# A two-expert MoE layer on one core: the experts last, their weighted rows added to the result in memory

## The chip, the cores and the metric

The kernel runs on one core of one Trainium2 chip. The time is the device time of that core in microseconds, from launch to end of one execution. The kernel before takes 1065.1 us, the median of three runs (1060.12, 1065.28 and 1065.1). Five engines matter: TensorE (PE in the profile; its weight loads are PEld), VectorE (DVE), ScalarE (ACT), GpSimd (POOL) and SyncE (SP). Each runs its own list of instructions strictly in order and waits on semaphores. DMAs are started from SyncE, ScalarE or GpSimd and are carried out by 16 DMA engines; a DMA whose rows are addressed by a list of indices (indirect) is started from GpSimd.

## The reference

Eight sequences of 256 tokens (2048 in all) of width 1024, float32. Each sequence has an adapter matrix; its product y goes through a mixture of experts with a shared part, and the result is added to x:

```python
y = einsum('bsi,boi->bso', x, cond_weight[itok])            # adapter by sequence
g, u = split(y @ shared_w_gate_up.T, 2)                     # 1024 each
shared = (silu(g) * u) @ shared_w_down.T
probs = softmax(y @ gate_w.T)                               # 16 experts
vals, idx = top_k(probs, 2); vals /= vals.sum(-1)
for each expert e:                                          # 256 inner, gate and up
    out_e = (silu(g_e) * u_e) @ w_down[e].T
out = x + shared + sum over the two experts of vals * out_e
```

## The kernel before

**Arithmetic.** Products are float32 in effect: each operand is split into a high and a low part (`split`, L58, a cast on ScalarE at L59 and a subtraction on VectorE at L60), and `mm3` (L73) makes three TensorE products for each. A weight tile of 128x1024 is loaded from SyncE into one of four `wst` buffers and split into one of seven `whl` buffers (`load_w`, L64).

**Stages.** The token blocks are 128 rows, and four of them make a group; there are four groups.

1. `cond` (L145), once for each sequence: y = adapter product, written to `y_d` in memory from ScalarE's queue.
2. `group_yt` (L469): reads y of a group back from GpSimd's queue and transposes it. `route` (L171): gate products, softmax, the two best experts, their weights `c1` and `c2`, and each token's rank within its expert. With it, indirect DMAs of one number a token scatter the token's place in `y_d` into a table `tab_d`, sorted by expert (L268). The index tile `sli` of that scatter has one buffer. A table of the weights goes to `comb_d`.
3. `shared_up` (L284) and `shared_down` (L307) for a group: 384 and 192 products. The order is group 0, interleaved with stages 1 and 2, then group 3, then the experts, then groups 1 and 2.
4. Before the experts, small VectorE work sorts the experts by their number of tokens and computes, for each token and each of its two experts, the row in `os_d` where that expert's output row will be (`s1i`, `s2i`, L546 to L556).
5. `experts` (L457) goes through the 16 experts, the fullest first. Each has a fixed capacity (`CAPS`, 304 down to 256 tokens). `expert_rows` (L431) loads the expert's table entries (`ib`) from SyncE, makes the addresses (`segments`, L425, on GpSimd) and gathers y in pieces of 128 rows x 256 (`gather_rows`, L345, L351). `expert_yt` transposes them, `expert_up` (L384) makes the 96 up products, `expert_down` (L396) and, for tokens from 256 on, `expert_down_last` (L412) make 24 or 32 down products. `expert_out` (L449) writes the rows to `os_d` from SyncE. On TensorE the up products of expert n+1 stand ahead of the down products of expert n. Output tiles `o` have three buffers, gathered rows `yg` four.
6. `combine` (L328) gathers, for a token block, the two rows from `os_d` (L331) and adds them with their weights on VectorE (L337). For groups 1 and 2 it adds into the tile that the shared network is then added to. Groups 0 and 3 had gone to `xs_d` before the experts; `combine_kept` (L339) reads them back, combines and writes them to `out`, between the up products of group 1 and of group 2.
7. Tokens beyond an expert's capacity are handled by `rest` (L579) in a loop at the end. With these inputs no expert has any.

**Order.** The program is written in this sequence; a scheduler, which is given a simulated timeline (L650), decides how instructions of different steps are interleaved on each engine. Buffers that are in use, and the last load (`issue_after`), hold later steps back.

Of the kernel before, what the change touches and what calls it, by code (L numbers as in the profile page):

```python
# [9 lines left out]
F32 = mybir.dt.float32  # L10
# [16 lines left out]
# tokens computed in the main pass for the fullest expert, the next one, ...; what is past them comes after it  # L27
# [4 lines left out]
ROW0 = [sum(CAPS[:n]) for n in range(E + 1)]  # L32
ZROW = ROW0[E]
PAD = 4 * T


@with_exitstack
def adapter_moe_kernel(ctx: ExitStack, tc: tile.TileContext, xT, x, itok, wc, gate, wgu, wd, sgu, sd, out):
# [14 lines left out]
    comb_d = dram.tile([T + P, E], F32, tag="comb_d", name="comb_d")  # L53
    tab_d = dram.tile([E * SLOTS, 1], I32, tag="tab_d", name="tab_d")
    os_d = dram.tile([ZROW + 16, H], F32, tag="os_d", name="os_d")
    xs_d = dram.tile([T, H], F32, tag="xs_d", name="xs_d")
# [27 lines left out]
    tid = cpool.tile([P, T // P], I32, tag="tid", name="tid")  # L84
    rev = cpool.tile([P, NB, E], F32, tag="rev", name="rev")
    caps = cpool.tile([P, E], F32, tag="caps", name="caps")
    row0 = cpool.tile([P, E], F32, tag="row0", name="row0")
    oneh = [cpool.tile([P, T // P, E], BF, tag=f"oneh{r}", name=f"oneh{r}") for r in range(2)]
    ranks = [cpool.tile([P, T // P], F32, tag=f"ranks{r}", name=f"ranks{r}") for r in range(2)]
    # hi/lo of the gate for each chunk; a stationary block runs on into the next chunks, whose products aren't used  # L90
    gpk = cpool.tile([P, (NC - 1) * 2 * E + P], FR, tag="gpk", name="gpk")
    s1i = cpool.tile([P, T // P], I32, tag="s1i", name="s1i")
    s2i = cpool.tile([P, T // P], I32, tag="s2i", name="s2i")
    c1 = cpool.tile([P, T // P], F32, tag="c1", name="c1")
    c2 = cpool.tile([P, T // P], F32, tag="c2", name="c2")
# [3 lines left out]
    def constants():  # L99
# [5 lines left out]
        nc.gpsimd.iota(tid, pattern=[[4 * P, T // P]], base=0, channel_multiplier=1)  # L105
# [6 lines left out]
        for j in range(E):  # L112
            nc.gpsimd.memset(row0[:, j : j + 1], float(ROW0[j] - ZROW))
# [12 lines left out]
        nc.sync.dma_start(comb_d[T : T + P, :], zr[:, :E])  # L126
        nc.sync.dma_start(os_d[ZROW : ZROW + 16, :], zr[:16, :])
        ti = rows.tile([P, 1024], I32, tag="yg", bufs=4, name="ti")
        nc.gpsimd.memset(ti[:, : E * SLOTS // P], PAD)
        nc.sync.dma_start(tab_d.rearrange("(p f) o -> p (f o)", p=P), ti[:, : E * SLOTS // P])  # L130

    # r: partition (a, i), column (t, c), 32 rows i of each t, segment a of 256 columns of a row
    # -> hi/lo of the transpose at columns off:off+n of yt [P, 2, NC, *]; partition (a, j) of
    # chunk b holds column 256a + 32b + j
# [36 lines left out]
    def route(g, yt):  # L171
# [44 lines left out]
        v.tensor_tensor(c1[:, gs], m[0], den, op=ALU.mult)  # L216
        v.tensor_tensor(c2[:, gs], m[1], den, op=ALU.mult)
        cb = t3("cb")
        v.tensor_tensor(cb, oh[0], bc(c1[:, gs]), op=ALU.mult)
        v.tensor_tensor(key, oh[1], bc(c2[:, gs]), op=ALU.mult)  # L220
        v.tensor_tensor(cb, cb, key, op=ALU.add)
        nc.scalar.dma_start(comb_d[g * GT : (g + 1) * GT, :].rearrange("(k p) e -> p k e", p=P), cb)
# [24 lines left out]
        for r in range(2):  # L247
            rank = ranks[r][:, gs]
            sl, sli, tq, ov, u = t2("sl"), t2("sli", I32), t2("tq"), t2("ov"), t2("u")
            v.tensor_copy(oneh[r][:, gs, :], oh[r])  # L250
            v.tensor_tensor(key, rk, oh[r], op=ALU.mult)
            v.tensor_reduce(rank, key, axis=AX.X, op=ALU.add)
            # place of rank 32t + i: 8i + t below MAIN, the rank itself from MAIN on
            v.tensor_scalar(ov, rank, float(MAIN), None, op0=ALU.is_lt)
            v.tensor_scalar(tq, rank, -15.5, 1.0 / 32, op0=ALU.add, op1=ALU.mult)
            v.tensor_copy(sli, tq)
            v.tensor_copy(tq, sli)
            v.tensor_scalar(u, rank, 7.0, None, op0=ALU.mult)
            v.scalar_tensor_tensor(u, tq, -255.0, u, op0=ALU.mult, op1=ALU.add)
            v.tensor_tensor(u, u, ov, op=ALU.mult)  # L260
            # expert = E - kk
            v.tensor_scalar(sl, kk[r], -float(SLOTS), float(SLOTS * E), op0=ALU.mult, op1=ALU.add)
            v.tensor_tensor(sl, sl, rank, op=ALU.add)
            v.tensor_tensor(sl, sl, u, op=ALU.add)
            v.tensor_copy(sli, sl)
            for k in range(NB):
                tb = g * NB + k
                nc.gpsimd.indirect_dma_start(  # L268
                    out=tab_d[:, :],
                    out_offset=bass.IndirectOffsetOnAxis(ap=sli[:, k : k + 1], axis=0),  # L270
                    in_=tid[:, tb : tb + 1],
                    in_offset=None,
                )
# [54 lines left out]
    def combine(tb, a):  # L328
        for si, cw in ((s1i, c1), (s2i, c2)):
            r = rows.tile([P, 1024], F32, tag="yg", bufs=4, name="r")  # L330
            nc.gpsimd.indirect_dma_start(  # L331
                out=r,
                out_offset=None,
                in_=os_d[:, :],
                in_offset=bass.IndirectOffsetOnAxis(ap=si[:, tb : tb + 1], axis=0),
            )
            nc.vector.scalar_tensor_tensor(a, r, cw[:, tb : tb + 1], a, op0=ALU.mult, op1=ALU.add)  # L337

    def combine_kept(tb):  # L339
        a = rows.tile([P, 1024], F32, tag="o", name="kept")  # L340
        nc.sync.dma_start(a, xs_d[tb * P : (tb + 1) * P, :])
        combine(tb, a)
        nc.sync.dma_start(out[tb * P : (tb + 1) * P, :], a)

# [51 lines left out]
    def expert_down(at, w, off):  # L396
        o = rows.tile([P, 1024], F32, tag="o", name="o")
        for h in range(2):
# [9 lines left out]
            nc.scalar.copy(o[:, h * 512 : (h + 1) * 512], ps)  # L408
        return o

    # a3: hi of n tokens at columns 0.., lo at 64..; the products' halves are added after
    def expert_down_last(a3, w, n):  # L412
        o = rows.tile([P, 1024], F32, tag="o", name="ol")
        for h in range(2):
# [6 lines left out]
            nc.vector.tensor_tensor(o[:n, hs], ps[:n, :], o[:n, hs], op=ALU.add)  # L421
        return o[:n, :]

    # ib: places in y of 32 rows for each t -> those of their four segments
# [5 lines left out]

    def expert_rows(n):  # L431
        e = expert_id(n)
        last = CAPS[n] - MAIN
        nt = -(-last // 32)
        ib = sml.tile([32, 10], I32, tag="ib", name="ib")
        nc.sync.dma_start(ib[:, :8], tab_d[ds(e * SLOTS, MAIN), :].rearrange("(i t) o -> i (t o)", t=8))
        for t in range(nt):
            nc.sync.dma_start(ib[:, 8 + t : 9 + t], tab_d[ds(e * SLOTS + (MAIN + 32 * t), 32), :])
        ix = segments(ib, 8 + nt)
# [9 lines left out]
    def expert_out(n, at):  # L449
        w = load_wd(expert_id(n))  # L450
        r0 = ROW0[n]
        for j in range(2):
            nc.sync.dma_start(os_d[r0 + j * P : r0 + (j + 1) * P, :], expert_down(at, w, j * P))
        if CAPS[n] > MAIN:
            nc.sync.dma_start(os_d[r0 + MAIN : r0 + CAPS[n], :], expert_down_last(at3[n % 2], w, CAPS[n] - MAIN))

    def experts(yt, rs, after):  # L457
        at = expert_up(0, yt)
        for n in range(E):
            yt = expert_yt(rs) if n + 1 < E else after()  # L460
            if n + 2 < E:
                rs = expert_rows(n + 2)
            prev = at
            if n + 1 < E:
                at = expert_up(n + 1, yt)
            expert_out(n, prev)
        return yt

    def group_yt(g):  # L469
        yt = big.tile([P, 2, NC, GT], FR, tag="big", name="yt")  # L470
        for k in range(NB):
            r = rows.tile([P, 1024], F32, tag="yg", bufs=4, name="yr")
            # token 4i + t of the block at (t, i)
# [19 lines left out]
    shared_down(0, ht, acc, xs_d, (0,))  # L493
# [6 lines left out]
    shared_down(0, ht, acc, xs_d, (1,))  # L500
    route(3, yt)
    # tokens per expert
# [13 lines left out]
    # experts by their number of tokens, the fullest first  # L516
    rev1 = rev[:, 0, :]
    cnt, pos, sq = once("cnt", [P, E]), once("pos", [P, E]), rows.tile([P, E, E], F32, tag="o", name="sq")
    perm, red, capof = once("perm", [P, E, E], BF), once("red", [P, E]), once("capof", [P, E])
# [6 lines left out]
    # perm[n, e]: expert e is the n-th  # L526
# [4 lines left out]
    v.tensor_tensor(sq, perm, by_row(caps[:, :]), op=ALU.mult)  # L531
    v.tensor_reduce(capof, sq.rearrange("p n e -> p e n"), axis=AX.X, op=ALU.add)
    # blocks of P tokens past its capacity, for the n-th, and their sum: ceil(k / P) = rint((k + 63.5) / P)
# [10 lines left out]
    # row of the experts' results, by token; the row of zeros for a rank past the capacity  # L544
    v.tensor_tensor(sq, perm, by_row(row0[:, :]), op=ALU.mult)
    v.tensor_reduce(pos, sq.rearrange("p n e -> p e n"), axis=AX.X, op=ALU.add)  # L546
    for r, si in enumerate((s1i, s2i)):
        lim, row = once("lim", [P, T // P]), once("row", [P, T // P])
        v.tensor_tensor(sq, oneh[r], by_col(capof[:, :]), op=ALU.mult)
        v.tensor_reduce(lim, sq, axis=AX.X, op=ALU.add)  # L550
# [103 lines left out]
```

## Time and profile before

| What | Value |
|---|---|
| runs | 1060.12, 1065.28, 1065.1 us; median 1065.1 |
| profiled execution | span 1060.8 us, from its first to its last instruction |
| TensorE | 1029.5 us busy, 5181 products; mean clock 0.992 |
| VectorE, ScalarE, GpSimd | 657.7, 466.4, 292.1 us busy |
| DMA | 243.86 MB, 230 GB/s in the mean |
| queue started from SyncE (q1) | 186.46 MB, 52.6% of the 16 engines' span |
| queue started from GpSimd (q0) | 47.87 MB, 13.0% |
| HBM | 203.11 MB read, 39.69 MB written |

The span is 0.7 us above the lowest run and 4.3 below the median. In the profile's lists, `L60 DVE TENSOR_TENSOR hl<-st,hl` is line 60's instruction on VectorE that writes `hl` from `st` and `hl`. Tiles: `st` and `hl` are weights as loaded and as split, `eps` and `ops` the experts' up and down sums, `sps` and `dps` those of the shared network, `cps` those of the adapters, `yte` an expert's transposed rows, `xacc` a block of x to which results are added. A busy TensorE counts a product from start to modelled end, so neighbours overlap; products of 512 columns follow one another every 0.23 us. In a table by stretches, the columns after the length are busy microseconds of each engine with the number of instructions, then the granted TensorE clock, the mean busy share of the DMA engines and GB/s.

### The profile page before, as it was taken

How to read it: one execution, taken by the hardware profiler on the slowest of the kernel's cores; microseconds unless marked ns; L12 is line 12 of the kernel's file. 1: busy time of each engine (PE TensorE's matmuls, PEld its weight loads, DVE VectorE, ACT ScalarE, POOL GpSimd, SP SyncE). 2: the span in 40 equal slices, each digit the busy share in tenths (PEclk: the TensorE clock that was granted, in tenths of full speed). 3: DMA queues.
4: the chain of work that ended last, by engine and by line, in shares of the span. 5: the costliest groups of instructions: out<-in, count | busy, mean ns of one | idle time of the engine just before them, and what ended most of it. 6: DMA issues, size and time to landing. Idle time of an engine off the chain costs nothing.

```text
span 1060.8 us, 14494 instructions
## 1 busy us (share of the span) xinstructions
PE 1029.5 (97%) x5181; PEld 875.8 (83%) x5181; DVE 657.7 (62%) x918; ACT 466.4 (44%) x626; POOL 292.1 (28%) x332
## 2 busy tenths in 40 slices
PE   6989999999899899999999999999999999999997
PEld 5877888888677688889999999989988888888886
DVE  5676543765567745546877878777784768537321
ACT  5564342544344423314667666566473233122200
POOL 1000210001200223644666656545203423002000
PEclk9999999999899999999999999999999999999999
DMA  7986384567677443655788888787979987827201
GB/s 257 345 301 219 105 253 140 204 232 215 223 249 253 135 159 88 220 189 186 237 283 275 291 271 282 249 273 251 340 262 358 408 344 264 318 92 258 80 33 50
DMA packets 82557, 243.86 MB, mean 230 GB/s; under 512 B 14204, under 2 KB 23164, under 8 KB 82476
## 3 DMA queue, kind: packets, MB, share of 16 engines
q1 hardware_dynamic: 56060, 186.46, 52.6%
q0 software_dynamic: 15856, 47.87, 13.0%
q10 hardware_dynamic: 10560, 8.52, 2.4%
q8 instruction: 42, 0.69, 0.2%
q14 instruction: 39, 0.32, 0.1%
HBM read 203.11 MB, written 39.69 MB: 229 GB/s over the span
## 4 chain that ended last, share of the span: by engine, by line
PE 57%; DMA 5%; issue 5%; POOL 3%; DVE 3%; ACT 1%; POOLq 0%; DVEq 0%; ACTq 0%
PE sps L76 8%; PE sps L75 8%; PE sps L74 8%; PE dps L76 4%; PE dps L75 4%; PE dps L74 4%; PE eps L76 4%; PE eps L74 4%; PE eps L75 4%; POOL yg L351 3%; PE ops L76 2%; PE ops L75 1%; DMA y_d<-yrow 1%; PE ops L74 1%; PE ops L419 1%
## 5 line engine op out<-in xcount | busy, mean ns | idle before, releaser
L60 DVE TENSOR_TENSOR hl<-st,hl 128x1024 fp32r<-128x1024 f32 (+1 forms) x274 | 330.1, 1209 | 180.0 <-ACT hl L59 178.9
L59 ACT CAST hl<-st 128x1024 fp32r<-128x1024 f32 (+1 forms) x274 | 283.5, 1043 | 254.8 <-PE sps L76 79.0
L76 PE MATMUL sps<-yt,hl 128*128 128x512 f32 x512 | 199.5, 390 | 0.0
L75 PE MATMUL sps<-yt,hl 128*128 128x512 f32 x512 | 199.4, 389 | 0.0
L74 PE MATMUL sps<-yt,hl 128*128 128x512 f32 x512 | 198.9, 390 | 0.0
L351 POOL DMA_INDIRECT yg<-y_d,ix x128 | 149.9, 1171 | 40.1 <-issue 35.1
L74 PE MATMUL eps<-yte,hl 128*128 128x256 f32 (+6 forms) x512 | 147.6, 289 | 0.1
L76 PE MATMUL eps<-yte,hl 128*128 128x256 f32 (+6 forms) x512 | 147.5, 288 | 0.0
L75 PE MATMUL eps<-yte,hl 128*128 128x256 f32 (+6 forms) x512 | 147.0, 287 | 0.0
L76 PEld LDWEIGHTS sps<-yt,hl 128*128 128x128 f32 x512 | 96.1, 188 | 20.0
L74 PEld LDWEIGHTS sps<-yt,hl 128*128 128x128 f32 x512 | 96.2, 188 | 19.9
L75 PEld LDWEIGHTS sps<-yt,hl 128*128 128x128 f32 x512 | 96.1, 188 | 19.9
L74 PE MATMUL cps<-hl 128*128 128x512 f32 x256 | 100.8, 398 | 7.6 <-ACT hl L59 7.6
L75 PE MATMUL cps<-hl 128*128 128x512 f32 x256 | 102.2, 399 | 3.2 <-DVE hl L60 3.2
L76 PE MATMUL cps<-hl 128*128 128x512 f32 x256 | 101.7, 397 | 0.0
L76 PE MATMUL dps<-hl,ht 128*128 128x512 f32 x256 | 99.8, 390 | 0.0
L75 PE MATMUL dps<-hl,ht 128*128 128x512 f32 x256 | 99.6, 389 | 0.0
L74 PE MATMUL dps<-hl,ht 128*128 128x512 f32 x256 | 99.6, 389 | 0.0
L74 PEld LDWEIGHTS eps<-yte,hl 128*128 128x128 f32 x512 | 96.4, 188 | 1.1 <-DVE s L378 0.5
L75 PEld LDWEIGHTS eps<-yte,hl 128*128 128x128 f32 x512 | 96.5, 188 | 0.7
L76 PEld LDWEIGHTS eps<-yte,hl 128*128 128x128 f32 x512 | 96.3, 188 | 0.0
L474 POOL DMA_DIRECT2D yr<-y_d x24 | 13.4, 559 | 239.9 <-DMA y_d<-yrow 189.7
(153 smaller groups left out, 1307.5 us busy)
## 6 DMA issues: line engine op xcount, KB each, us to landing
st<-sgu SPq DMA_DIRECT2D x64, 512.0 KB, 3.7
st<-wgu SPq DMA_DIRECT2D x64, 512.0 KB, 3.8
st<-wc SPq DMA_DIRECT2D x63, 512.0 KB, 4.7
st<-sd SPq DMA_DIRECT2D x32, 512.0 KB, 3.9
st<-wd SPq DMA_DIRECT2D x32, 512.0 KB, 5.2
os_d<-o SPq DMA_DIRECT2D x32, 512.0 KB, 5.7
yr<-y_d POOLq DMA_DIRECT2D x24, 512.0 KB, 6.3
y_d<-yrow ACTq DMA_DIRECT2D x16, 512.0 KB, 8.9
```

Of the source, the lines that this page charges most:

```text
L59: nc.scalar.copy(hi, src)
L60: nc.vector.tensor_tensor(lo, src, hi.bitcast(F32), op=ALU.subtract)
L74: nc.tensor.matmul(ps, lhs[0], rhs[0], start=first, stop=False)
L75: nc.tensor.matmul(ps, lhs[0], rhs[1], start=False, stop=False)
L76: nc.tensor.matmul(ps, lhs[1], rhs[0], start=False, stop=last)
L351: nc.gpsimd.indirect_dma_start(out=r[:, t * 256 : (t + 1) * 256], out_offset=None, in_=y_d.rearrange("k a p f -> (k a p) f"), in_offset=ba ...
L419: nc.tensor.matmul(ps, a3[:, fi, :], w[fi][:, l, hs], start=(fi == 0 and l == 0), stop=(fi == 1 and l == 1))
L474: nc.gpsimd.dma_start(r, y_d[g * NB + k].rearrange("a (i t) f -> (a i) (t f)", t=4))
```

## The change

The experts come after all four groups of the shared network. The order is group 0, 3, 1, 2, then the experts, the one with the fewest tokens first. All shared results go to `out` at once; `xs_d`, `os_d`, `comb_d`, `combine` and `combine_kept` are gone.

A table entry grows from one number to four (`ENT`): the token's place in `y_d`, its weight for this expert, its row in `out`, and an unused one. Empty entries name one of 256 extra rows (`DUMMY`) at the end of `out`, which the result leaves out. The table is in plain order of rank, and the step that permuted ranks below 256 is gone. Before the experts, `entries` loads the numbers of all 16 experts from SyncE (two or three DMAs for each): the places with 32 to a column (`ibs`), and whole entries with one to a partition (`ews`).

`expert_down` scales by the weight when ScalarE copies the sums out; `expert_down_last` multiplies on VectorE. `add_out` then starts, from GpSimd, an indirect DMA that adds the tile's rows to rows of `out` in memory. An expert's adds wait for all adds of the expert before it; those of one expert do not wait for each other. In the built order the adds of an expert stand on GpSimd among the gathers of later experts.

The core of the diff:

```diff
-    tab_d = dram.tile([E * SLOTS, 1], I32, tag="tab_d", name="tab_d")
-    os_d = dram.tile([ZROW + 16, H], F32, tag="os_d", name="os_d")
-    xs_d = dram.tile([T, H], F32, tag="xs_d", name="xs_d")
+    tab_d = dram.tile([E * SLOTS, ENT], I32, tag="tab_d", name="tab_d")
...
+        for r in range(2):
+            v.tensor_tensor(ent[r][:, :, :].bitcast(F32)[:, gs, 1], m[r], den, op=ALU.mult)
...
-                    in_=tid[:, tb : tb + 1],
+                    in_=ent[r][:, tb, :],
...
-            nc.scalar.copy(o[:, h * 512 : (h + 1) * 512], ps)
+            nc.scalar.activation(o[:, h * 512 : (h + 1) * 512], ps, AF.Copy, scale=cw)
...
+        nc.vector.tensor_scalar(o[:n, :], o[:n, :], cw, None, op0=ALU.mult)
         return o[:n, :]
...
+    def entries(ib, ew, base, nt):
+        nc.sync.dma_start(ib[:, :nt], tab_d[ds(base, 32 * nt), 0:1].rearrange("(t i) o -> i (t o)", i=32))
+        nj, m = divmod(nt, 4)
+        nc.sync.dma_start(ew[:, :nj, :], tab_d[ds(base, P * nj), :].rearrange("(j p) o -> p j o", p=P))
+        if m:
+            nc.sync.dma_start(ew[: 32 * m, nj, :], tab_d[ds(base + P * nj, 32 * m), :])
...
+    def add_out(o, ew, j, n=P):
+        i = nc.gpsimd.indirect_dma_start(
+            out=out,
+            out_offset=bass.IndirectOffsetOnAxis(ap=ew[:n, j, 2:3], axis=0),
+            in_=o,
+            in_offset=None,
+            compute_op=ALU.add,
+        ).ins
+        for k in adds[0]:
+            tc.add_manual_dep(i, k.name, SYNC, reason="adds to the same rows")
+        for k in adds[1]:
+            tc.declare_no_dep(i, k, reason="different rows")
+        adds[1].append(i)
...
     def expert_out(n, at):
         w = load_wd(expert_id(n))
+        ew = ews[:, n]
+        next_adds()
         for j in range(2):
-            nc.sync.dma_start(os_d[r0 + j * P : r0 + (j + 1) * P, :], expert_down(at, w, j * P))
+            add_out(expert_down(at, w, j * P, weight(ew, j)), ew, j)
...
+    ns = list(range(E))[::-1]
...
-    yt = experts(yt, rs, lambda: group_yt(1))
...
+    def shared(g, yt, prepare):
+        ht = shared_up(yt, up_tile())
         acc = down_rows(g)
+        after = prepare()
         shared_down(g, ht, acc, out)
+        return after
+
+    yt = shared(3, yt, lambda: group_yt(1))
+    yt = shared(1, yt, lambda: group_yt(2))
+    for n in ns:
+        entries(ibs[:, n], ews[:, n], expert_id(n) * SLOTS, 8 + last_tiles(n))
+    rs = expert_rows(ns[0])
+    yt = shared(2, yt, lambda: expert_yt(rs))
+    experts(yt, expert_rows(ns[1]))
```

## The prediction

> **What bounds the kernel now.** I read the page's first two parts (who is busy, and when), then a table of stages, then the chain that ended last, then GpSimd's own timeline, since the change moves work onto it.
>
> ```profile
> span 1060.8 us, 14494 instructions
> PE 1029.5 (97%) x5181; PEld 875.8 (83%) x5181; DVE 657.7 (62%) x918; ACT 466.4 (44%) x626; POOL 292.1 (28%) x332
> DMA  7986384567677443655788888787979987827201
> ```
> TensorE is busy for 97% of the span; the other engines have room as averages. The DMA row is in tenths of the 16 engines: it is near 8 in the expert stage (slices 19 to 29) and 9 just after it.
>
> ```profile
> core 0: us, PE busy (x) PEld busy (x) DVE busy (x) ACT busy (x) POOL busy (x), PEclk, DMA share, GB/s
> 256.00:276.00 20.00, 17.35 (x65) 13.73 (x64) 7.81 (x12) 7.90 (x9) 3.61 (x3) 0.83 0.60 188
> 583.00:636.00 53.00, 53.00 (x357) 49.59 (x356) 40.75 (x54) 33.91 (x57) 32.83 (x37) 1.00 0.85 283
> 689.00:742.00 53.00, 53.00 (x364) 49.03 (x364) 38.59 (x45) 34.21 (x54) 26.82 (x32) 1.00 0.81 263
> 742.00:795.00 53.00, 51.30 (x327) 45.48 (x326) 41.88 (x43) 32.78 (x49) 6.96 (x9) 1.00 0.86 299
> 795.00:848.00 53.00, 53.00 (x235) 43.88 (x235) 31.65 (x31) 16.95 (x22) 20.85 (x15) 1.00 0.98 382
> 1007.00:1061.00 54.00, 47.29 (x209) 38.84 (x207) 10.49 (x13) 2.63 (x3) 0.00 (x0) 0.96 0.11 41
> ```
> In the expert stage (477 to about 790) TensorE has no gap and a full clock, so nothing is gained there by relieving another engine. Its 31.3 us of idle time lie at the start, in the routing stage (53 to 106 and 265 to 371), 1.7 us where experts hand over to the shared network, and 6.7 us at the end. The block combine (gathers of `os_d`, 795 to 975) runs under a full TensorE: it fills the DMA (0.98) and costs TensorE nothing.
>
> ```profile
> 560.30 1.86 PE ops L419 x8
> 580.04 1.86 PE ops L419 x8
> 599.77 1.86 PE ops L419 x8
> 593.63 1.15 POOL L428 TENSOR_SCALAR ix<-ib 32x9 int32<-32x9 int32 x4 [2.43 <-DMA ib<-tab_d]
> 606.54 1.61 POOL L351 DMA_INDIRECT yl<-y_d,ix  x1 [0.30 <-issue]
> 613.27 1.12 POOL L428 TENSOR_SCALAR ix<-ib 32x9 int32<-32x9 int32 x4 [5.11 <-DMA ib<-tab_d]
> r<-os_d,s1i POOLq DMA_INDIRECT x16, 7.7
> 1054.33 0.69 DVE L325 TENSOR_TENSOR xacc<-dps,xacc 128x512 f32<-128x512 f32 x1 [0.67 <-PE dps L76]
> ```
> The first three lines (chain) give an expert's period: 19.7 us. The next three (GpSimd's timeline) give its part: from 593.63 to 608.15 it issues one expert's gathers, 14.5 us, then it is free for 5.1. The issue row says that an indirect 512 KB gather lands 7.7 us after its issue. The last line is the last compute; TensorE ended at 1054.31, 6.5 us before the span.
>
> **What goes.** 32 gathers of `os_d`, 32 multiply-adds on VectorE (20.6 + 20.2 us), eight reloads of `xs_d` and eight extra writes of `out`, about 30 MB of traffic, lie under a TensorE without a gap: worth 0. So are the routing instructions removed (per block of tokens some 22 of 0.15 to 0.2 us): they end no TensorE wait that I find. The routing stall at 256 to 276 comes from the index tile `sli`, which waits for four scatters one behind another (a wait of 8.44 us on VectorE, then half clock: 2.65 us idle and 17% of the clock, about 6 us in all). In the new order the second `sli` again stands behind the first with four weight splits between, as before, and the scatters are still four in a row: it stays. At route(2) two re-reads of `y_d` now stand among the scatters, which can hold VectorE some 7 us longer; three split weight tiles (24 matmuls of 0.23 us each, 16.8 us) cover that. Sum of both: 0, with 5 either way in the range.
>
> **What is added, off the path.** 43 small loads of table entries on SyncE during the shared stages: at 0.33 us an issue, 14 us of a queue that is otherwise waiting for a free weight buffer (502 us of waits on VectorE's splits); landing 3.6 to 4.9 us like the old `ib` loads; needed some 90 us later. 0; without the cover each group of nine would hold one weight load by about 5 us. The weights now come in by the scale of ScalarE's eviction (0.585 us with or without, by the COPY row: 0) and by one VectorE multiply of 8 to 48 rows x 1024 in eleven experts; the 128x1024 multiply-add took 1.28, the 0.67 for each existing half bounds it below: about 0.7 us of VectorE, which is busy 41 of 53: 0. The 43 writes of `os_d` leave SyncE, where they waited 41.6 us for ScalarE; no weight load came too late for that, so 0. The gap of 1.7 us at 742 to 795 goes with the old handover: -1.
>
> **What is added on GpSimd.** 43 accumulating scatters. No row shows one. Below: the gathers of `os_d`, also 128 rows of 4 KB: 0.96 us (s2i median) + 0.30 gap = 1.26. Above: [...]the slow form of the row (1.68, s1i median), 1.5 x 1.68 + 0.3 = 2.8. I take 1.68 + 0.3 = 2.0. In the built order the adds of an expert stand among the gathers for the fifth expert after it. The first five experts (256 tokens, two adds) meet gathers of nine: 14.5 + 4.0 = 18.5 against a period of 17.5 (120 of the 364 matmuls in 689 to 742): 1.0 over. The next six (three adds): 14.5 + 6.0 = 20.5 against 19.5: 1.0 over. After that there are no gathers. 11 us late in all, of which the lead of the gathers hides some: they are issued about two periods (39 us) before their transposes need them, 18 us of it are used, 8 is landing: 13 us of cover. But output tiles are three: the third add of an expert is issued 18.5 us after its down products begin, lands 8 later, and ScalarE wants the buffer back at 26.7. Lateness there stands in front of the weight copies on ScalarE, which have about one expert's up-projection (12 us) of split weights ahead of TensorE. So 11 us late costs about 3. By 1.26: 0. By 2.8: 2.6 x 5 + 3.4 x 6 = 33, less 10 of cover: 23.
>
> The first add of an expert also waits until all of the one before have landed. One turn on GpSimd is landing L of the third add + 2 (first add) + 5 (four gathers) + 2 + 1.6 + 2 = L + 12.6. The third add is small; the nearest row is `yl` with 4.1, the far one 7.7. At 4.1 to 6.9 it fits the period; at 7.7 it adds 0.8 a turn for six turns, 5 us. I take 0 beyond the 3 above. What waits behind it is the gathers, and behind these VectorE's transposes.
>
> **What is added on the DMA.** In the trace's packet records one of 4 KB takes 159 ns in the median (16 engines: 412 GB/s). An expert's 1.1 MB of output is 17 packets on each engine: 2.7 us when written. Here a page speaks against the change: the Trainium skill, "Collectives: The Full Stack", section "The bandwidth ceiling: the fold count and why AG ≠ RS ≠ AR", says that an add in the DMA fetches two sources for each thing written, so that it runs at half the rate of a copy. By the rows alone the adds replace plain writes of the same bytes and the DMA share stays 0.85: sum 0. By the page, estimated, 2.7 us more in 19.5: 0.85 + 0.14 = 0.99, as full as 795 to 848, where weight loads landed after 6.7 to 15 us instead of 3.8. Weight loads have four buffers and seven split tiles ahead, so a late landing is mostly absorbed. No run here shows an add; I take the page's factor and 3 us for it. At three fetches' worth it would be 1.13: 2.5 us a period, 40 in all.
>
> **The end.** The last 64 products are the down steps of the last two experts, 64 x 0.2325 = 14.9 us. From their start: the third tile of the first one is evicted and scaled at about 10 (7.4 + 0.58 + 0.67 + 0.7 and a queue); its add lands L1 later; only then the last expert's three adds go, 1.5 apart, and the last lands L2 after its issue: 10 + L1 + 3 + L2. For an otherwise idle DMA I take 6 and 6, between the least of the `os_d` gathers (4.1) and their median (7.7): 25, that is 10 after TensorE ends. Before, 0.7 + 3.6 (landing of `out<-xacc`) = 4.3. So +6; at 4.1 each +2, at 7.7 each +9. Another rule: the skill's "DMA: Bandwidth & Descriptors", section "Anatomy of one DMA — SWDGE (gpsimd) path", gives 2.0 us + bytes at 436 GB/s: 2.4 us for 192 KB, with which the chain of waits no longer shows and the end is as long as before: 0 instead of +6. The row of this trace decides: 7.7 against the rule's 3.2 for 512 KB.
>
> **Sum.** 0 + 0 - 1 + 3 + 3 + 6 = +11 on the profiled 1060.8, which is 0.7 above the lowest run and 4.3 below the median 1065.1. On the median: 1076; I say 1075.
>
> **Rivals.** (B) The DMA or GpSimd becomes the bound of the expert stage: the share of 0.85 with a second fetch, and 14.5 us of 19.5 already issued, speak for it; the free 5 us and deep weight buffers against. +20 to +45 and +6 at the end: 1085 to 1112. (C) The accumulate is not pipelined, each row's fetch waits for the one before: 17 rows an engine at 1 us, 17 us in place of 2.7, makes a period of about 31: +180 and more, 1245. Nothing here speaks for it but that no row excludes it. (D) All of it is hidden but the end, and that lands as by the shorter rows: +2 to +5, 1064 to 1070. (E) Faster: the routing stall of 6 us goes, because the shorter index chain starts the four scatters early enough. It decides if they land 8.4 us earlier than at 266.4; the chain is shorter by about 2.3, and one weight split fewer stands ahead. With the end at 0 and the handover: 1065.1 - 6 - 2 = 1057.
>
> **How the numbers follow.** A (this sum, 1068 to 1088) 0.46, B 0.25, C 0.09, D 0.14, E 0.06. 0.5% (1059.8 to 1070.4) is about what a measurement of this kernel tells from no change. Faster 0.06; same D and a little of A, 0.20; slower 0.74. The range 1063 to 1112 leaves out E, C and some of B's top, 0.18.[...]
>
> **What would show it.** A: TensorE without gaps in the expert stage, an end some 12 us after its last product with a wait of GpSimd for its own adds; scatters of about 1.7 us. B: DMA share 1.0 or GpSimd without idle there, weight copies waiting for `st<-wgu`, or ScalarE's evictions for adds. C: packets of the software queue far over 320 ns. D and E: the end under 9 us; no clock below 1 at 256 to 276. I am wrong if the adds land in over 12 us or take over 2.8 us to issue.

## The result and the profile after

The changed kernel takes 1134.0 us (median of 4, 1131.8 to 1136.1) beside 1064.0 us for the kernel before: ratio 1.065, 95% interval 1.062 to 1.068, slower. The forecast was 1075 with a range of 1063 to 1112, so the sign was right and the size far too small; even the rival in which GpSimd or the DMA becomes the bound ended at 1112.

From the first two parts of the page of the changed kernel:

```profile
span 1133.8 us, 14307 instructions
PE 1049.5 (93%) x5181; PEld 891.2 (79%) x5181; DVE 612.4 (54%) x797; ACT 471.4 (42%) x626; POOL 349.0 (31%) x337
...
PE   6999999999799999999999999999998677778994
...
PEclk9999999999899999999999999999999888898898
DMA  7985574766776444644346343568987767767775
```

TensorE is as full as before up to three quarters of the span and then has holes, with a lower clock in the same slices. Its idle time is 1133.8 - 1049.5 = 84.3 us in place of 31.3: 53.0 more. Its busy time is 20.0 us longer for the same 5181 matmuls, which is the clock. 53 + 20 = 73 is the whole loss.

The stages of the changed kernel (us, PE busy, PEld, DVE, ACT, POOL, granted clock, DMA share, GB/s):

```profile
795.00:848.00 53.00, 53.00 (x376) 49.73 (x375) 37.86 (x45) 34.66 (x52) 37.80 (x34) 1.00 0.91 271
848.00:901.00 53.00, 44.09 (x261) 38.21 (x261) 29.79 (x41) 23.66 (x39) 36.89 (x32) 0.90 0.74 206
901.00:954.00 53.00, 40.14 (x232) 36.91 (x231) 27.43 (x39) 23.91 (x39) 39.36 (x32) 0.84 0.70 193
954.00:1007.00 53.00, 40.63 (x246) 37.74 (x245) 27.48 (x37) 24.15 (x38) 38.65 (x31) 0.87 0.70 186
1007.00:1060.00 53.00, 41.13 (x232) 37.91 (x231) 28.53 (x39) 23.77 (x39) 38.27 (x29) 0.87 0.73 196
```

Four stages of 53 us, 848 to 1060, hold 46.0 of the 53.0 us of new idle time; all stages ahead of them are as full as forecast. The DMA share falls there from 0.91 to 0.70, so a full DMA is not what holds. TensorE is down to 40 to 44 of 53 us, VectorE and ScalarE to 24 to 30. GpSimd (POOL) is busy for 37 to 39 us in some 30 instructions, each followed by a gap of 0.3, so that some 47 of the 53 us are taken. One turn of GpSimd's timeline shows it, from the second add of one expert to the second add of the next:

```profile
962.59 1.64 POOL L421 DMA_INDIRECT out<-o,ews  x1 [0.31 <-issue]
964.53 0.98 POOL L319 DMA_INDIRECT yl<-y_d,ix  x1 [0.30 <-issue]
965.81 1.38 POOL L421 DMA_INDIRECT out<-ol,ews  x1 [0.31 <-issue]
970.59 1.15 POOL L397 TENSOR_SCALAR ix<-ibs 32x9 int32<-32x9 int32 x4 [3.40 <-DMA yl<-y_d,ix]
972.01 1.95 POOL L319 DMA_INDIRECT yg<-y_d,ix  x1 [0.27 <-POOL ix L397]
974.26 1.75 POOL L319 DMA_INDIRECT yg<-y_d,ix  x1 [0.30 <-issue]
976.32 3.48 POOL L319 DMA_INDIRECT yg<-y_d,ix  x1 [0.30 <-issue]
980.10 2.31 POOL L319 DMA_INDIRECT yg<-y_d,ix  x1 [0.30 <-issue]
982.72 2.29 POOL L421 DMA_INDIRECT out<-o,ews  x1 [0.30 <-issue]
985.32 1.68 POOL L319 DMA_INDIRECT yg<-y_d,ix  x1 [0.30 <-DVE hl L60]
987.30 0.96 POOL L319 DMA_INDIRECT yg<-y_d,ix  x1 [0.30 <-issue]
988.56 0.95 POOL L319 DMA_INDIRECT yg<-y_d,ix  x1 [0.31 <-issue]
989.81 0.95 POOL L319 DMA_INDIRECT yg<-y_d,ix  x1 [0.30 <-issue]
991.06 1.63 POOL L421 DMA_INDIRECT out<-o,ews  x1 [0.30 <-issue]
```

The turn is 28.5 us where TensorE needs 19.7 for an expert. Three adds take 5.3, eight gathers 14.0, one gather of the short block 1.0, the index instructions 1.2, gaps 3.6, and one true wait 3.4, in which `ix` waits for the landing of the `yl` gather issued 6 us earlier. GpSimd is never idle but for that. Eight turns in a row, 829 to 1048, take 25.2 to 28.7 us. They are not all alike: the first two have two adds and gathers of 9.1 in all, as short as in the kernel before, and stand at `ix` for 6.8 and 5.5.

The chain that ended last tells another story of the same stretch:

```profile
933.91 7.69 DMA out<-o,ews
...
941.71 0.69 ACT o L376
...
956.85 0.84 POOL yg L319
...
962.59 7.46 DMA out<-o,ews
```

It runs from the landing of an add (7.7 us) to ScalarE's eviction into the same output tile, by casts and transposes to GpSimd's gathers, and to the next add. The list of waits has both (us in total, times, the longest):

```profile
ACT o L376 <- DMA out<-o,ews: 92.8, 17, 9.4
POOL ix L397 <- DMA yl<-y_d,ix: 32.5, 8, 6.8
```

The first is the longest new wait. Read alone, it says that three output tiles are too few. Which of the two sets the turn is what the experiments had to tell.

The end, on TensorE and on GpSimd:

```profile
1116.69 2.01 PE L387 MATMUL ops<-hl,at 128*128 128x512 f32 x8
...
1118.82 1.57 POOL L421 DMA_INDIRECT out<-o,ews  x1 [3.70 <-ACT ol L388]
1120.69 1.61 POOL L421 DMA_INDIRECT out<-o,ews  x1 [0.30 <-issue]
1122.61 1.37 POOL L421 DMA_INDIRECT out<-ol,ews  x1 [0.31 <-issue]
```

TensorE ends at 1118.7, 15.1 us before the span does; before it was 6.5. That is 8.6 of the loss.

### The profile page after: what moved, and what is told of

Its sections match the earlier page's. It is cut to its first block, busy times and chain, and to the rows that moved or that the text cites. A ratio compares the mean times of both kernels' runs of the same rounds, so it can differ in the third digit from the quotient of the medians.

```text
span 1133.8 us, 14307 instructions
## 1 busy us (share of the span) xinstructions
PE 1049.5 (93%) x5181; PEld 891.2 (79%) x5181; DVE 612.4 (54%) x797; ACT 471.4 (42%) x626; POOL 349.0 (31%) x337
## 4 chain that ended last, share of the span: by engine, by line
PE 46%; DMA 9%; POOL 9%; issue 8%; DVE 3%; ACT 2%; POOLq 0%; ACTq 0%; DVEq 0%
PE sps L76 8%; PE sps L75 8%; PE sps L74 8%; POOL yg L319 5%; PE dps L76 4%; PE dps L75 4%; PE dps L74 4%; DMA out<-o,ews 4%; PE eps L74 3%; PE eps L76 3%; PE eps L75 3%; POOL out L421 2%; DMA yr<-y_d 2%; DMA tab_d<-ent,sli 2%; DVE tt L139 1%
## 5 line engine op out<-in xcount | busy, mean ns | idle before, releaser
L319 POOL DMA_INDIRECT yg<-y_d,ix x128 | 174.1, 1360 | 286.3 <-DVE tt L139 248.7
L74 PE MATMUL eps<-yte,hl 128*128 128x256 f32 (+6 forms) x512 | 155.0, 303 | 38.9 <-ACT o L376 36.6
L76 PE MATMUL eps<-yte,hl 128*128 128x256 f32 (+6 forms) x512 | 152.8, 299 | 0.0
L75 PE MATMUL eps<-yte,hl 128*128 128x256 f32 (+6 forms) x512 | 152.7, 298 | 0.0
L74 PEld LDWEIGHTS eps<-yte,hl 128*128 128x128 f32 x512 | 102.4, 200 | 42.8 <-ACT o L376 38.1
L76 PEld LDWEIGHTS sps<-yt,hl 128*128 128x128 f32 x512 | 96.1, 188 | 19.8
L75 PEld LDWEIGHTS eps<-yte,hl 128*128 128x128 f32 x512 | 102.2, 200 | 0.4
L76 PEld LDWEIGHTS eps<-yte,hl 128*128 128x128 f32 x512 | 101.8, 199 | 0.0
```

The lines of the kernel that those rows point to most:

```text
L74: nc.tensor.matmul(ps, lhs[0], rhs[0], start=first, stop=False)
L75: nc.tensor.matmul(ps, lhs[0], rhs[1], start=False, stop=False)
L76: nc.tensor.matmul(ps, lhs[1], rhs[0], start=False, stop=last)
L319: nc.gpsimd.indirect_dma_start(out=r[:, t * 256 : (t + 1) * 256], out_offset=None, in_=y_d.rearrange("k a p f -> (k a p) f"), in_offset=ba ...
```

## The experiments

In all of them but the one with the fullest expert first, the order of instructions on TensorE and ScalarE is that of the changed kernel, and on the other engines too apart from what the edit itself moves, so that times can be laid side by side. Medians drift by some us from one set of runs to the next (the kernel before: 1061.8 to 1067.6), so the table goes by the ratio to the kernel before on the same chip. Each median is of two to five executions.

| kernel | us | ratio, 95% |
|---|---|---|
| changed kernel | 1134.0 | 1.065 (1.062 to 1.068) |
| seven output tiles | 1126.4 | 1.059 (1.055 to 1.063) |
| own rows for each expert | 1130.9 | 1.064 (1.058 to 1.070) |
| plain scatter | 1096.2 | 1.031 (1.026 to 1.036) |
| two index tiles in the routing | 1135.6 | 1.066 (1.060 to 1.072) |
| indices ahead | 1090.3 | 1.023 (1.019 to 1.027) |
| indices ahead, seven output tiles | 1078.8 | 1.012 (1.009 to 1.015) |
| four `ix` buffers, seven output tiles | 1105.5 | 1.037 (1.033 to 1.041) |
| less work on VectorE | 1103.1 | 1.032 (1.026 to 1.038) |
| indices ahead, `yl` three tiles, outputs four | 1091.2 | 1.021 (1.016 to 1.027) |
| the same, fullest expert first | 1094.6 | 1.024 (1.020 to 1.029) |
| indices ahead, seven tiles, plain scatter | 1075.3 | 1.007 (1.005 to 1.009) |
| indices ahead, seven tiles, own rows | 1081.5 | 1.014 (1.011 to 1.016) |

### Is it the output tiles, the wait between experts, or the add itself?

Seven output tiles:

```diff
-        o = rows.tile([P, 1024], F32, tag="o", name="o")
+        o = out_tile("o")
```

`out_tile` takes the three tiles of `o` and the four of `xa`, free by then, in turn.

> The experts' output tiles are taken from two tags in turn (three tiles of `o`, four of `xa`): seven in place of three, the order of every engine's instructions unchanged. Theory R (the ring through the output tiles: ScalarE, in order, waits for an add to land before it can evict the next tile, and the casts, transposes and gathers stand behind it): the waits `ACT o <- DMA out<-o,ews` (92.8 us) fall under 10, TensorE's 46 us of idle time between 848 and 1060 and some 20 us of lowered clock go, the end stays: 1066 to 1080. Rival G (GpSimd's own turn: the first add of an expert waits on GpSimd's queue for all adds of the one before, with the gathers behind it): a turn of 20 to 23 us stays in place of 28.5, 1085 to 1100. Rival D (the second fetch of the add loads the DMA): no change, over 1120.

Measured 1126.4. The 92.8 us of ScalarE's waits are gone from the stretch, and the ratio moved by 0.6% only, 1.065 to 1.059. R, the theory that I held, falls as the main cause; G's number is missed too, for the turn is still 26.8 us; D's stands. But GpSimd's timeline now shows what none had counted:

```profile
943.40 5.47 POOL L406 TENSOR_SCALAR ix<-ibs 32x9 int32<-32x9 int32 x4 [2.15 <-DMA yl<-y_d,ix]
949.15 1.93 POOL L319 DMA_INDIRECT yg<-y_d,ix  x1 [0.28 <-POOL ix L406]
```

Four instructions of 32 x 9 elements, 1.15 us in the turn above, take 5.5; the wait for `yl` is 2.1; the gathers are down to 9.7. VectorE's wait for `yl` is 86.9 us in place of 9.4. One cost went and others took its place, and the turn of GpSimd's queue stayed.

Own rows:

```diff
-            out=out,
+            out=dst if dst is out else dst[:, :],
...
-        for k in adds[0]:
+        for k in adds[0] if dst is out else []:
...
-            add_out(expert_down(at, w, j * P, weight(ew, j)), ew, j)
+            add_out(expert_down(at, w, j * P, weight(ew, j)), ew, j, dst=own[n])
```

> Each expert adds into a memory region of its own (what is left out: the sum over the experts in one result), so that no add waits for those of the expert before; order, sizes and output tiles as they were. R: an add still has to land before its tile is free, so the stretch of 848 to 1060 keeps its period of some 28 us; the end is 5 us shorter: 1115 to 1130. G: the turn on GpSimd falls to its 20.5 us of issues: 1070 to 1090. D: no change but the end, 1120 to 1130.

Measured 1130.9, 1.064: no difference from the changed kernel. The wait of the first add for the adds of the expert before is not what sets the turn, which kills G as I had put it. The end after the last product is 12.1 us in place of 15.1.

Plain scatter:

```diff
-            compute_op=ALU.add,
```

> The scatters overwrite the rows in place of adding to them (what is left out: the addition), with all waits as they were. D (the second fetch): software-queue packets of 4 KB fall from a mean of 258 ns to about 185, and the stretch comes back to 19.7 us an expert: 1065 to 1085. R: what counts is the landing, 7.5 to 10 us for an add; a plain scatter of 512 KB is expected to land in 5 to 7, and each turn to be shorter by 2 to 4 us: 1100 to 1120. G: the same 2 to 4 us a turn, and the issue 0.3 shorter: 1100 to 1115.

Measured 1096.2, better than R and G had it and short of D. The turn with three adds is 24.2 to 24.5 us: the scatters 4.2 in place of 5.3 (1.04 us in the median and not 1.63), the gathers 12.0 in place of 14.0, the wait for `yl` 2.5 in place of 3.4. These make up the 4 us that the turn lost, so about half of the loss goes with the addition, by way of GpSimd's queue. D's own sign came true without its time: in the trace's packet records the software queue's packets of 4 KB take 182 ns in the mean in place of 258, and TensorE still lacks 20.8 us in 848 to 1060. Why the gathers are shorter too these runs do not settle.

### GpSimd's own queue

With R, G and D all missed, the theory Q was formed: GpSimd's in-order queue, with its stretched instructions and its wait for `yl`, is the bound. Then taking something off that queue must give back just that much.

```diff
     def expert_rows(n):
...
-        ix = segments(ibs[:, n], 8 + nt)
+        ix = ixs[:, n]
...
+    for n in ns:
+        segments(ibs[:, n], 8 + last_tiles(n), ixs[:, n])
```

> The index tiles of all sixteen experts are computed once, ahead of the experts (one tile of 16 x 10 indices in place of two buffers in turn), so that GpSimd no longer stands at `ix` until the last `yl` has landed; three output tiles as in the changed kernel, and the rest of the order unchanged. Theory Q (GpSimd's own queue is what paces the stretch: 28.5 us a turn = gathers 13.9 + adds 5.3 + `yl` 1.0 + `ix` 1.1 + wait for `yl` 3.5 + gaps 3.6): the turn falls by 4.6 to 24, over eight turns 35 us: 1095 to 1110. Theory R (the output tiles): GpSimd has time to spare, the turn is set by the landing of the adds, so no more than 10 us are won: 1120 to 1134.

Measured 1090.3, 44 us back where 35 were worked out; below Q's range by 5 and far from R's. All that was moved is sixteen sets of four tiny instructions, and the wait with them. The 35 were one turn's 4.6 times eight; over the eight turns the list of waits has 32.5 us at `ix`, and the `ix` instructions there take 12.7, so 45 in all, and that came back. The turn is 22.0 to 24.9 with three adds, and 16.3 to 21.6 with two.

Both edits together, `ix = ixs[:, n]` and `out_tile`:

> Both edits, the indices ahead and seven output tiles. Q: the turn of 26.8 us that was measured with seven tiles loses the `ix` of 5.5 and the wait of 2.1: 19.2, which is under TensorE's 19.7; no idle time of TensorE is left between 848 and 1030, and what remains over the kernel before is the end: 1066 to 1078. If the DMA or the adds' own landing set a floor (D): a turn of 23 and more, over 1090.

Measured 1078.8, just past the top of Q's 1066 to 1078. By the ratios, output tiles are worth some 12 us here and 6 above: they are a part, the smaller one. The stages of this kernel:

```profile
848.00:901.00 53.00, 53.00 (x364) 49.57 (x363) 36.37 (x49) 32.68 (x51) 41.49 (x31) 1.00 0.88 263
901.00:954.00 53.00, 51.05 (x321) 45.69 (x320) 40.53 (x56) 33.03 (x55) 44.47 (x29) 1.00 0.89 256
954.00:1007.00 53.00, 49.95 (x320) 45.12 (x318) 35.27 (x47) 30.74 (x50) 40.15 (x29) 1.00 0.84 240
1007.00:1060.00 53.00, 51.06 (x295) 45.42 (x295) 34.74 (x51) 30.90 (x52) 24.38 (x13) 1.00 0.77 192
```

46 us of idle time are now 6.9 (none was forecast), and the clock is 1.00 throughout. GpSimd is as busy as ever in 901 to 954: it stands at its limit still, with turns of 18.3 to 23.7 us.

The same with more buffers only:

```diff
-        ix = sml.tile([P, 10], I32, tag="ix", name="ix")
+        ix = sml.tile([P, 10], I32, tag="ix", name="ix", bufs=4)
```

> Seven output tiles, and four buffers for `ix` in place of two: the wait for the last `yl` goes, but the `ix` instructions stay between the gathers. Q: the turn of 26.8 us loses the 2.1 of waiting for sure; `ix` itself stays long (5.5 us for four instructions of 32 x 9) if VectorE's work at that moment is what holds it, 24.7 a turn and 1105 to 1118; if it was only long because it started together with VectorE after the landing, it falls to about 1.2 and the turn to 20.4: 1070 to 1085.

Measured 1105.5, at the edge of the first of the two ranges. Three of the turns are still 27.1 to 28.4 us, with an `ix` of 5.4 to 5.5 us and a wait for `yl` of 2.4 to 3.8 in front of it, which was expected to go; the turns around them are 20.7 to 23.4. The built order shows why: with four buffers `ix` runs further ahead of the gathers, and by the count of instructions its buffer is then again one last read by a `yl` gather issued just before, since `yl` has a single buffer and lags behind. What cures it is that `ix` is out of the queue, not its buffers.

### What stretches GpSimd's instructions

Laid against VectorE's records, the gathers of the slow stretch (925 to 1040) take 0.96 us in the mean where VectorE is busy for less than a fifth of the gather, and 2.09 where it is busy for over four fifths (11 and 22 gathers). The longest gather of a turn, and VectorE's timeline beside it and its neighbours:

```profile
947.88 3.46 POOL L319 DMA_INDIRECT yg<-y_d,ix  x1 [0.30 <-issue]
943.36 1.23 DVE L60 TENSOR_TENSOR yte<-tt,yte 128x1024 fp32r<-128x1024 f32 x1 [10.59 <-ACT yte L59]
944.56 0.68 DVE L389 TENSOR_TENSOR ol<-ops,ol 8x512 f32<-8x512 f32 x1
945.17 0.42 DVE L139 STREAM_TRANSPOSE tt<-yl 128x256 f32<-128x256 f32 x1
945.53 1.20 DVE L60 TENSOR_TENSOR hl<-st,hl 128x1024 fp32r<-128x1024 f32 x1
...
948.65 0.73 DVE L390 TENSOR_SCALAR ol<-ol,ews 8x1024 f32<-8x1024 f32 x1
949.31 1.21 DVE L60 TENSOR_TENSOR hl<-st,hl 128x1024 fp32r<-128x1024 f32 x1
```

VectorE stood for 10.6 us and then has all its work in one heap, with a single gap of 0.26 us until after 958: the same wait that delays it makes it press on the gathers afterwards. To try it, the heap was made smaller:

```diff
-            split(hl[:, 0, cs], hl[:, 1, cs], st[:, cs])
+            nc.scalar.copy(hl[:, 0, cs], st[:, cs])
+            cl = slice(cs.start, min(cs.stop, cs.start + part))
+            nc.vector.tensor_tensor(hl[:, 1, cl], st[:, cl], hl[:, 0, cl].bitcast(F32), op=ALU.subtract)
```

`part` is 128 of 1024 columns for the up weights and 512 for the down weights.

> The changed kernel with less work on VectorE in the expert stage alone: the low halves of the experts' weights are computed for 128 of 1024 columns (up) and 512 of 1024 (down), and those columns are used for all products (what is left out: most of the low halves of the expert weights; the number and shape of the matmuls stay). VectorE loses about 4.7 us of some 17 an expert; the order on the other engines is unchanged. Theory V (the gathers on GpSimd are long, 1.6 us in the mean and up to 4.2, because VectorE runs without a gap beside them; 0.96 where it is idle): the eight gathers of a turn fall from 13.9 us to 10 or 11, and the turn from 28.5 to 24 to 25.5: 1100 to 1118. If it is the DMA queue or the packets that hold the gathers (D): they stay at 13 to 14 and the time within 1128 to 1136.

Measured 1103.1. The same four gathers of a turn (L321 is the gather's line here):

```profile
975.35 1.04 POOL L321 DMA_INDIRECT yg<-y_d,ix  x1 [0.27 <-POOL ix L399]
976.69 0.96 POOL L321 DMA_INDIRECT yg<-y_d,ix  x1 [0.30 <-issue]
977.96 1.12 POOL L321 DMA_INDIRECT yg<-y_d,ix  x1 [0.30 <-issue]
979.38 1.71 POOL L321 DMA_INDIRECT yg<-y_d,ix  x1 [0.31 <-issue]
```

In the turns with three adds the eight gathers sum to 8.7 to 9.7 us in place of 11.1 to 14.1, and the turn is 23.3 to 24.3 in place of 25.7 to 28.7: what the gathers lost, the turn lost, and TensorE's idle time between 848 and 1060 is 19.8 us in place of 46.0. V holds, and D's "13 to 14" is out. A dense VectorE alone does not do it: in this kernel it has no gap either between 975.4 and 982, but its `hl` splits are 0.3 to 0.7 us there and not 1.2.

One rival inside V stands open. L390 above is the change's own multiply by the weight, which the prediction priced at 0, and in six turns of the changed kernel the gather beside it is the longest, 3.4 to 4.2 us, while the two turns without it have none above 1.9; in the run with seven tiles a single `ix` instruction beside it takes 3.7 to 3.8 in five turns, and 0.24 elsewhere. With less work on VectorE the multiply is still there, and the gather beside it takes 1.3 to 1.9. So most of the length goes with the splits around it; the multiply was not moved by itself.

### Cheaper still, and the rest

`yl` in the three tiles of `o`, outputs in the four of `xa`:

```diff
-            r = rows.tile([P, 512], F32, tag="yl", name="yl", bufs=1)
+            r = rows.tile([P, 1024], F32, tag="o", name="yl")
...
-        o = rows.tile([P, 1024], F32, tag="o", name="o")
+        o = rows.tile([P, 1024], F32, tag="xa", name="o", bufs=4)
```

> Indices ahead as before; the short third blocks of gathered rows (`yl`, one tile) get the three tiles of `o`, and the experts' outputs the four tiles of `xa`. Beside the run with seven output tiles (1078.8) this takes away VectorE's wait for `yl` (32.6 us in 8 times) but leaves four output tiles. Q: TensorE's idle time of 6.9 us between 901 and 1060 goes for the most part: 1071 to 1077; if four tiles are too few (R), waits of ScalarE for `out<-o` come back, 10 us or more in all: 1080 to 1090.

Measured 1091.2, just past the second case: `ol`'s evictions wait 25.3 us for landings of adds, six times, so R's mechanism is real. That it is the price of this run is not shown: TensorE's idle time between 371 and 1060 is 13.1 us in place of 6.9, and 5.9 of it lie ahead of 848 in short gaps for which the profile names nothing.

The same with the order of experts of the kernel before:

```diff
-    ns = list(range(E))[::-1]
+    ns = list(range(E))
```

> The run before it with the experts in the order of the kernel before, the fullest first, so that the last ones have two adds and no third tile. The end after TensorE's last product (15.1 us in the changed kernel, 6.5 before) loses one add of 1.4 us, the gap, and a third tile's eviction: 11 to 13, so 2 to 4 us faster than the run beside it, 1068 to 1075. If the turns with three adds now cost more at the start: no gain or a few us slower.

Measured 1094.6: a miss. The end got longer, 21.8 us after the last product at 1073.0, and GpSimd's timeline tells why:

```profile
1059.62 1.56 POOL L423 DMA_INDIRECT out<-o,ews  x1 [9.75 <-DMA out<-o,ews]
...
1070.14 1.55 POOL L423 DMA_INDIRECT out<-o,ews  x1 [7.10 <-ACT o L376]
...
1080.44 1.55 POOL L423 DMA_INDIRECT out<-o,ews  x1 [6.90 <-ACTq L583]
```

The adds of the last three experts go some 10.4 us apart (two adds 3.4, a landing 6.9 to 7.1). In the last two lines the brackets name ScalarE and its queue, but the rows of the add at 1070.14 had been ready since 1065.3, and what ended there, by the trace's semaphores, was the landing of the adds before. Adds that lag can't catch up faster than that, while ScalarE has the sums of the last two experts ready 5.6 us apart (1068.1 and 1073.7). TensorE itself ends within 1 us of the run beside it (1072.1).

Last, on the kernel of 1078.8, the two edits from above: no `compute_op`, and a region of memory for each expert.

> The kernel with indices ahead and seven output tiles (1078.8), its scatters overwriting in place of adding (what is left out: the addition). GpSimd's queue is no longer the limit there, or just, so that what the second fetch of the add costs on the DMA and on GpSimd stands by itself. By the forecast's term for the DMA (3 us) with an end about 2 us shorter: 1072 to 1075. If the second fetch costs nothing once the queue is cured: only the end, 1076 to 1078. If it is what fills TensorE's remaining 6.9 us of idle time in that stretch, as a GpSimd instruction of 1.04 in place of 1.65 us too: 1067 to 1072.

Measured 1075.3, beside 1078.8 with the add, and the end 10.5 us after the last product in place of 15.2. The end by itself, 4.7 us shorter, is the whole gain (3.5 us by the medians, 5 by the ratios); for the stages nothing is left that these runs could tell. The fetch itself is there: page part 3, the same packets and bytes, with the add and without it.

```profile
q0 software_dynamic: 16352, 48.97, 18.0%
```
```profile
q0 software_dynamic: 16352, 48.97, 12.7%
```

18.0% of 1080.7 less 12.7% of 1077.9 is 57.6 us of all 16 engines, 3.6 us an expert. At the end, where the software queue carries nothing but these rows, a packet of 4 KB takes 328 ns with the add and 162 without it, in the median.

> The same kernel with a memory region for each expert (what is left out: the sum over the experts), so that no add waits for those of the expert before. The forecast's term for the end had 6 us in it for the landing of the adds of the last expert but one; with three output tiles own rows shortened the end from 15.1 to 12.1 us after the last product. So 3 us faster, 1074 to 1077, if the wait between experts counts at the end alone; 1068 to 1073 if GpSimd's queue also stands behind it in the turns before.

Measured 1081.5: a miss. The end is 12.5 us in place of 15.2, but the total is no shorter. In this profile TensorE lost 2.9 us between 742 and 795, where the run without own rows lost none with the same order of instructions, so 3 us are under what these runs tell apart.

The two index tiles, an aside on the routing stage:

```diff
-            sl, sli = t2("sl"), t2("sli", I32)
+            sl, sli = t2("sl"), t2(f"sli{r}", I32)
```

> The two index tiles of the routing's scatters get a buffer each in place of one for both. The stall in the routing stage (VectorE's wait of about 8 us for four scatters at some 266 us, and TensorE's half clock after it) goes: 4 to 8 us faster than the changed kernel, 1126 to 1130, with the expert stage as it was. If the stall has another cause: the same as the changed kernel.

Measured 1135.6, no gain. VectorE's wait for `sli` (6.2 us in the changed kernel) is gone and its transposes wait longer for the re-reads of `y_d` that stand behind the same scatters on GpSimd's queue: from 10.7 to 14.6 us.

```profile
DVE tt L139 <- DMA yr<-y_d: 14.6, 1, 14.6
```

The scatters into one table go one behind another, and somebody waits for them whichever tile is doubled.

## Why the prediction was wrong, by its steps

**The step that failed** is in "What is added on GpSimd": "14.5 + 6.0 = 20.5 against 19.5: 1.0 over", and what was made of it, "11 us late costs about 3". The turn is 25.2 to 28.7, eight times, and that is 46 us of idle time and 20 of clock. Term by term, for the turn of 28.5 shown above:

- The adds: 2.0 us each was right (1.63 and 1.39 in the median, and 0.3). 5.3 + 0.9 = 6.2 for the 6.0. It was a choice between two bounds, though, not a working: the plain scatter takes 1.04, not 1.68, and the add 1.57 times that.
- The 14.5 is 18.8 of the same instructions now: the gathers' mean was 1.20 in the old expert stage (530 to 640) and is 1.65 (925 to 1040). The row of the old turn was copied as if it were a constant. It depends on what VectorE does beside it, and the change made VectorE's work come in heaps.
- The wait of 3.4 was not in the sum; over the eight turns it is 32.5 us, more than what the gathers grew by (98 us for 64, where 73 would have been 9.1 for each eight). In the old turn GpSimd was "free for 5.1", and the bracket of that very line said `<-DMA ib<-tab_d`: it was a wait at `ix`, which I took as room. In the new order the same place waits for `yl`, issued just before it, with a landing of 6 us that nothing hides, since `ix` has two buffers, and the one to be written next was last read by that gather.

6.2 + 18.8 + 3.4 = 28.4. With cover of 13 us once, and 7 to 9 us lost in each turn, the lead was gone in the second turn; it was treated as if it covered the whole, as one sum of 11 us would be. (For an add of 2.8 the prediction itself took 10 for the same cover.)

**The rival B** named the right place, and one of its signs (ScalarE's evictions waiting for adds, with GpSimd without idle). Its price, 20 to 45, stood on an add of 2.8 us (23) or three fetches (40); the adds were cheap and the rest of the queue was not.

**The output tiles**: the mechanism was told ("Lateness there stands in front of weight copies on ScalarE") and it is there, 6 to 12 us; it was priced at 3 together with the rest. "A turn is L + 12.6" for the wait between experts: it sets nothing in the stretch, as forecast (own rows leave the turns at 25.3 to 29.6).

**The DMA**: the factor of two fetches, which the prediction took over from a collective's add, holds here (328 ns a packet for 162), and comes to 3.6 us an expert where 2.7 was estimated. The cost in time was not 3 but nothing that can be seen once the queue is relieved: with indices ahead and seven tiles the share is 0.84 to 0.97 from 795 to 1007, near the 0.99 estimated, and TensorE goes on. That deep weight buffers absorb late loads was not tried. In the changed kernel itself the share fell, as the stage was slowed by something else.

**The end**: +8.6, forecast +6; the mechanism as told (three adds, two landings), with 3.0 of it the wait for the expert before. By the trace's semaphores the last add lands 25.4 us after the start of TensorE's last 14.9, where 25 were worked out. What was left out is the 4.6 us from there to the end of the span. The 4.3 taken for the kernel before leaves out 2.2 us in the same way: the prediction's own line had 6.5. The rule that would have made it 0 (2.0 us + bytes at 436 GB/s, 3.2 for 512 KB) is far off in this loaded kernel (seven tiles, indices ahead; count and us from issue to landing last):

```profile
out<-o,ews POOLq DMA_INDIRECT x32, 8.5
```

**What cost nothing** did so: the combine and its traffic (24.8 MB less, for the "about 30"), the small loads on SyncE, the routing (12.3 us idle between 265 and 371, 11.5 before), the handover's 1.7 us back. ScalarE's eviction with a scale is 0.687 us, not 0.585; it does not show. The one term put at 0 that may not be is VectorE's multiply, as said above.

No version here beats the kernel before. The nearest with the whole computation is 1.2% slower, and 8.7 us of that is the end.

## What to carry to other kernels

Before work is put on an in-order queue, add up one whole turn of it, waits included, and ask of each idle bracket what it waits for: time at a wait for a landing is not room. Durations of a queue's instructions are those of the old neighbours; if the change makes another engine stop and then run in a heap, they are no longer valid. When two chains explain the same stretch, the longest wait in the list need not be the bound: give each its relief alone, and believe the one that gives the time back.

## What was not expected of the hardware

GpSimd's indirect gathers, 0.95 us to issue, took 2.09 in the mean (up to 3.5) beside a VectorE that was busy for over four fifths of them, and four tiny index instructions took 5.5 us in place of 1.2; with the weight splits of VectorE cut to a fraction the gathers beside a VectorE as busy took 1.20. The Trainium skill, "SBUF — State Buffer", section "Who interferes with whom", says that a VectorE instruction with two SBUF inputs holds up a GpSimd instruction that reads SBUF, which fits the index instructions; that such a `tensor_tensor` does not hold up the making of descriptors is inferred there. These gathers, which also read their indices in SBUF, were held, but which part of a gather is held is not settled by these runs, and in the kernel before the same density of VectorE cost less (1.3 in the mean).

Idle time of TensorE cost twice: with 17 to 24% of idle time in a stage the granted clock fell to 0.84 to 0.90, and the 46 us of holes brought 20 us of slower matmuls. With 4 to 6% of idle time in a stage (indices ahead, seven tiles) it stayed at 1.00. The share alone does not set it: the changed kernel shows 0.97 at 4% in 53 to 106, and indices ahead alone shows 1.00 at 10% in 954 to 1007.
